# Four graph layers on one core: a tenth buffer for the token tile, the value bias moved into a shared buffer, and a new order of the same instructions

## The chip, the cores and the metric

The kernel runs on one core of one Trainium2 chip. The metric is the device time of one launch in microseconds (us). The core has a matrix engine (TensorE, PE in the profile), three engines for elementwise work (VectorE or DVE, ScalarE or ACT, GpSimd or POOL) and a queue (SyncE, SP) from which all transfers between memory and the core are issued. Each engine runs its own instructions in the order in which the program lists them, and waits where an operand isn't ready yet.

## The reference, cut to what matters

128 graphs of 64 nodes with 512 numbers per node pass through four layers. Each layer normalizes its input, applies ReLU, mixes the nodes of a graph with a 64 x 64 matrix made from `adj`, multiplies by weights, and adds the result to the input.

```python
# layer 0
h = jnp.maximum(_layernorm(x), 0.0)
x = x + _L0_gnn_ref(h, adj, ...)      # two hypergraph convolutions, 512 -> 1024 -> 512
# layer 1
h = jnp.maximum(_layernorm(x), 0.0)
x = x + _L1_gnn_ref(h, adj, ...)      # A @ h @ w, A from tanh, exp and row sums
# layer 2
h = jnp.maximum(_layernorm(x), 0.0)
x = x + _L2_gnn_ref(h, adj, ...)      # weight = adj * exp(query keyt); weight @ value
#    value = h @ Wv_w.T + Wv_b        <- the bias "bv" of this text
# layer 3
h = jnp.maximum(_layernorm(x), 0.0)
x = x + _L3_gnn_ref(h, adj, ...)      # H = sum over k of (transition^k h) @ Wk[k] + bk[k]; relu
```

## The kernel before

The 8192 nodes are cut into 16 groups of four tiles of 128 nodes. The first half of the program takes every group through layers 0 and 1 and stores the four x tiles to memory (`xm`); the second half loads them again and takes every group through layers 2 and 3. The weights of the second half are loaded over those of the first when these are no longer needed.

The program isn't written in the order in which it runs. Each operation is put into a graph with an engine, a rough cost and a priority. A list scheduler then walks the graph with its own rough clock, gives every buffer a place out of a fixed number when its first operation starts, and lists each engine's instructions in the order that this walk found. Transfers wait for a place to come free.

```python
SLOTS = {
    "x": ([P, D], 9), "adj": ([P, 2, T, C], 3), "h": ([P, D], 5), "o": ([P, D], 2),
    ...
}
TWO = [                                   # the same memory, first half / second half
    ([("tmp", [P, D], 4), ("mB", [P, T, C + 1], 1)], [("s3", [P, 3, 6, P], 1)]),
    ...
    ([("y", [P, D], 2)], [("qT", [P, 2, 2 * P], 2)]),
    ...
]
```

A place on the right side of `TWO` can be given out only when all uses of the left side are over. Where the scheduler's clock shows a gap of over half a microsecond on TensorE, and a PSUM buffer is free, it puts in matmuls of ones whose result nobody reads (fills), so that the engine doesn't stand still:

```python
    gap, (since, i) = t - at["PE"], min(free["ps"], default=(t, 0))
    if o.eng == "PE" and gap > 0.5 and since <= at["PE"]:
        fills.append((o.seq, slots["ps"][i], gap))
...
def fill(ps, gap):
    for _ in range(int(gap * FILL / (0.224 if filled else 0.448))):
        nc.tensor.matmul(ps[:, :P], ones, ones, start=True, stop=True)       # L1013
    filled.append(gap)
```

An fp32 matmul of the program is two instructions in the profile. The priorities of an operation are a running count (`G.prio`), which grows by a period per group and by stretches within a layer, plus an offset per part of a layer (`AT`):

```python
STRETCH, PERIOD1, PERIOD2 = (2.11, 6.43, 4.5, 0.21), 79.8, 140.53
AT = {"x0": -1458.56, "apart": 58.27, "w1": -1207.06, ...}
def part(name):
    G.shift = AT[name]
```

Products of a weight with a pair of tiles are done in seven block products in place of eight (Strassen-Winograd): `strassen` makes sums of tile blocks on VectorE and then multiplies.

```python
def comb(d, kd, x_, kx, y_, ky, op):                                     # L599
    dve(c_v(kc * P), lambda: nc.vector.tensor_tensor(d(), x_(), y_(), op), [*kx, *ky], kd)
...
            nc.tensor.matmul(p.t[:, :n], lhsT()[:, c, :], rhs(c), ...)   # L607 (layer 2: L845)
...
comb(s1, ...); comb(s2, ...); comb(a[1, 0], ...); comb(s4, ...)
seven({1: prod(a11), 2: prod(a12), 3: prod(s4), 4: prod(a22), 5: prod(s1), 6: prod(s2), 7: prod(a21)}, U, n, emit)
```

The seven products run in the order 1, 6, 7, 2, 5, 4, 3. Four quarters of the result come out after the 2, the 5, the 4 and the 3. Some lines that the profile names (cut; line numbers are those of the kernel before):

```python
dma(256, lambda: nc.sync.dma_start(xx.t, at), key, [xx])                 # L344 x of a tile
pe(..., q_ @ k_, ...)                                                    # L467 Wq times Wk, set-up
nc.vector.bn_stats(st.t[:, i, :], src(i))                                # L516 mean, variance
nc.scalar.activation(h.t, xx.t, AF.Relu, bias=nm.t, scale=rs.t)          # L537 h of a tile
nc.tensor.matmul(quad(p)[:, c, :], h.t[...], rhs(), ...)                 # L546, copied by L548
nc.scalar.copy(planes, src)                                              # L555 before a DMA transpose
nc.sync.dma_start_transpose(back, planes)                                # L556, copied by L557
nc.tensor.matmul(pmv()[:, t, :], HT.t[:, t, :], mB.t[:, t, :], ...)      # L705 layer 0's node matrix
nc.tensor.matmul(pf.t, M.t[:, t, :], y.t, ...)                           # L758 end of layer 0, reads y
nc.vector.tensor_mul(PT.t[s, :, s], z.t[s], by_node(rn, s))              # L787 layer 1's node matrix
nc.tensor.matmul(quad(pl)[s, ...], hT.t[...], q()[...])                  # L878 logits of layer 2
nc.tensor.matmul(p.t, PT.t[:, t, :], v_.t[:, t % 2, c0:c1])              # L911 layer 2's output
nc.vector.transpose(tt.t[...], tr.t[...])                                # L948 layer 3's node matrix
nc.tensor.matmul(p2.t[...], tr.t[:, t, :], tt.t[:, t, 0, :])             # L957 its square
nc.tensor.matmul(quad(pqs[k][i])[:, c, :], hh[k].t[half, ...], tt...)    # L973
nc.vector.scalar_tensor_tensor(xx.t[:, cols], U.t[:, iv], 0.0, xx.t[:, cols], ...)  # L992 end of layer 3
dma(256, lambda: nc.sync.dma_start(out[r:r + P, :], xx.t), ...)          # L995
```

The bias of v has a buffer of its own, loaded once. It is used in layer 2 alone:

```python
bv_b = const.tile([P, D], F32, name="bv_b")
dma(256, lambda: nc.sync.dma_start(bv_b, bv.partition_broadcast(P)), [], ["bv_b"])    # L1055
```

Of the kernel before, what the change touches and what calls it, by code (L numbers as in the profile page):

```python
# [8 lines left out]
F32 = mybir.dt.float32  # L9
# [5 lines left out]
P = 128  # L15
C = 64
D = 512
DH = 1024
T = 4
# [148 lines left out]
def tile_adj_preln_d4(  # L168
# [6 lines left out]
    nc = tc.nc  # L175
# [3 lines left out]
    const = ctx.enter_context(tc.tile_pool(name="const", bufs=1))  # L179
# [3 lines left out]


    SLOTS = {
        "x": ([P, D], 9), "adj": ([P, 2, T, C], 3), "h": ([P, D], 5), "o": ([P, D], 2),
        "u5": ([P, 3, D], 2), "u2": ([P, 3, D // 2], 1),
        "bd": ([P, T, P], 4), "rw": ([P, C, T], 1), "ee": ([P, T, C], 2),
        "st": ([P, 2, 6], 6), "mv": ([P, 2], 10), "ve": ([P, 1], 10), "rs": ([P, 1], 10), "nm": ([P, 1], 10),
# [5 lines left out]
        ([("z", [P, DH], 2)], [("hT", [P, KD, T * P], 1)]),  # L195
        ([("rT", [P, KH, P], 3)], [("vu", [P, 2, D + 1], 2), ("tt", [P, T, 2, C], 2)]),
        ([("s2", [P, 3, 4, P], 1), ("s1", [P, 3, 2, P], 2)], [("a3", [P, 3 * KD, P], 2)]),
        ([("y", [P, D], 2)], [("qT", [P, 2, 2 * P], 2)]),
        ([("mT", [P, KD, P], 3)], [("a3", [P, 3 * KD, P], 1)]),
        ([("row", [P, D], 4)], [("sh", [P, 4, 2, 2 * P], 1)]),  # L200
        ([("wa", [P, D], 1)], [("q", [P, D], 1)]),
# [5 lines left out]
    def size(shape):  # L207
        n = 1
        for d in shape[1:]:
            n *= d  # L210
        return n

    for two in TWO:
        both = work.tile([P, max(sum(size(shape) * n for _, shape, n in tags) for tags in two)], F32,
                         name="_".join(tag for tags in two for tag, _, _ in tags))
        for tags in two:
            at = 0
            for tag, shape, n in tags:
                for i in range(n):
                    v = both[:, at:at + size(shape)]  # L220
                    at += size(shape)
                    if len(shape) == 3:
                        v = v.rearrange("p (a b) -> p a b", a=shape[1])
                    elif len(shape) == 4:
                        v = v.rearrange("p (a b c) -> p a b c", a=shape[1], b=shape[2])
# [30 lines left out]
    def c_v(n, from_psum=False):  # L256
        return n / 960 + 0.155 + 0.05 * from_psum
# [4 lines left out]
    def dve(cost, fn, r, w):  # L262
        return G.op("DVE", cost, fn, r, w)
# [4 lines left out]
    def pool(cost, fn, r, w):  # L268
        return G.op("POOL", cost, fn, r, w)

    def dma(kb, fn, r, w, issue=0.34):
        return G.op("SP", max(kb / 380.0, issue), fn, r, w)

    def quad(b):
# [2 lines left out]
    FILL = 0.75  # L277


    STRETCH, PERIOD1, PERIOD2 = (2.11, 6.43, 4.5, 0.21), 79.8, 140.53  # L280
    AT = {
        "x0": -1458.56, "apart": 58.27, "w1": -1207.06, "b1": -1268.61, "w2": 312.2, "w": -214.25, "c1": 103.95,
        "l0": -1592.46, "c2": -560.69, "l1": 125.29, "c": 849.04, "g0": -1279.86, "g1": -1456.39, "g2": -589.08,
        "g3": -1259.16, "g": -1258.76, "bq": 321.93, "l3": 56.2, "wg": 1603.23, "w3": 387.13, "beg0": -72.8,
        "beg1": 73.58, "end00": 0.51, "end01": 19.09, "end11": -75.14, "new2": 31.64, "new3": 4.77, "end2": -39.58,
        "end3": -21.31, "load1": -108.19, "load2": 27.97, "m": 12.29, "h0": 9.53, "p0": 10.98, "z0": -29.14,
        "q0": 15.48, "y0": -518.61, "h1": -26.33, "p1": -22.59, "z1": -30.25, "q1": 4.48, "y1": -2.94, "s": -20.64,
        "t0": -25.67, "e0": -522.9, "t1": -42.32, "e1": -53.88, "hT": 8.77, "sh": 220.05, "lq": 8.14, "pt": -124.53,
        "v": 35.92, "pv": -915.5, "s3": 19.84, "tt": -865.12, "a0": 46.62, "b0": -371.48, "a1": 104.26, "b1_": 198.72,
    }  # L290

    def part(name):
        G.shift = AT[name]
# [31 lines left out]
    def load_tmp(tag, n, shape_of, src):  # L325
        b = Buf(tag)
        dma(n * P * 4 / 1024, lambda: nc.sync.dma_start(shape_of(b.t), src), [], [b])
        return b
# [74 lines left out]
    def combine_hT(name, w_, x_, left):  # L403

        blk = lambda i, j: w_[:, 2 * i:2 * i + 2, j * D // 2:(j + 1) * D // 2]
        low, high = [(name, 0)], [(name, 1)]
        V = name + "V"
        add, sub = nc.vector.tensor_add, nc.vector.tensor_sub  # L410
        f = lambda i: (lambda c, o=slice(0, D // 2): x_[:, i, c, o])
        b = lambda i, j: (lambda c, o=slice(0, D // 2): blk(i, j)[:, c, o])
        v = lambda fn, r, w: dve(c_v(D), fn, r, w)
        if left:
            v(lambda: add(x_[:, 0], blk(0, 1), blk(1, 1)), [*low, *high], [(name, "x0")])
            v(lambda: sub(x_[:, 1], x_[:, 0], blk(0, 0)), [*low, (name, "x0")], [(name, "x1")])
            v(lambda: sub(x_[:, 2], blk(1, 0), x_[:, 1]), [*high, (name, "x1")], [(name, "x2")])
            v(lambda: sub(blk(0, 1), blk(0, 0), blk(0, 1)), [*low, (name, "x0")], [V])
        else:
            v(lambda: add(x_[:, 1], blk(1, 1), blk(0, 1)), [*low, *high], [(name, "x1")])  # L420
            v(lambda: sub(blk(0, 1), blk(0, 0), blk(0, 1)), [*low, (name, "x1")], [V])
            v(lambda: sub(x_[:, 0], blk(1, 1), blk(0, 1)), [*high, V], [(name, "x0")])
            v(lambda: sub(x_[:, 2], blk(1, 0), x_[:, 0]), [*high, (name, "x0")], [(name, "x2")])
        N = name + "N"
        v(lambda: nc.vector.tensor_scalar(blk(1, 1), blk(1, 1), -1.0, None, op0=ALU.mult), [*high, (name, "x0"), (name, "x1")], [N])
        x = lambda i: (f(i), [(name, f"x{i}")])
        if left:
            return {1: (b(0, 0), low), 2: (b(1, 0), high), 3: x(2), 4: (b(1, 1), [N, *high]), 5: x(0), 6: x(1), 7: (b(0, 1), [V])}
        return {1: (b(0, 0), low), 2: (b(1, 0), high), 3: (b(1, 1), [N, *high]), 4: x(2), 5: (b(0, 1), [V]), 6: x(0), 7: x(1)}
# [103 lines left out]
    def pre_ln(g, t, stats=None):  # L533

        xx, h = xt[g, t], Buf("h")
        nm, rs = stats or pre_stats(g, t)
        act(0.82, lambda: nc.scalar.activation(h.t, xx.t, AF.Relu, bias=nm.t, scale=rs.t), [xx, nm, rs], [h])  # L537
        return h
# [271 lines left out]
    def layer2(g):  # L810
        ad = adjs[g]
        part("hT")
        hT = Buf("hT")
        hk = [(hT, t) for t in range(T)]
        for t in range(T):
            h = pre_ln(g, t)
# [16 lines left out]
        pair = lambda f: f.rearrange("p (a n) -> p a n", a=2)  # L833
# [58 lines left out]

        def emit_v(i, j, p, u, v):
            cols, at = slice(j * D // 2, (j + 1) * D // 2), slice(j * (D // 2 + 1), j * (D // 2 + 1) + D // 2)
            bias = bv_b[:, None, cols].to_broadcast([P, 2, D // 2])
            add, ka = (lambda: bias), "bv_b"
            if u is not None:
                (U, iu), iv = u, v[1]
                pool(1.3, lambda: nc.gpsimd.tensor_add(pair(U.t[:, iv]), pair(U.t[:, iu]), bias), [u, "bv_b"], [v])
                add, ka = (lambda: pair(U.t[:, iv])), v  # L900
            dve(c_v(D), lambda: nc.vector.tensor_add(vb[i].t[:, :, at], pair(p.t), add()), [p, ka], [(vb[i], j)])


        hv = {**hs, 3: hs[4], 4: hs[3], 5: hs[7], 7: hs[5]}
        seven({n: prod(WV[n], hv[n], False) for n in range(1, 8)}, Buf("u5"), D, emit_v)
        PTk = [(PT, 0), (PT, C)]
        part("pv")
        for t in range(T):
# [6 lines left out]
            for j in range(2):  # L915
                cols = slice(j * D // 2, (j + 1) * D // 2)
# [134 lines left out]
    load_w("wg", wg_sb, wg_d, olds("w1", KD), ["wg_d"])  # L1051
    load_w("wv", wv_sb, WvT, olds("w1", KD))
    WG, WV = combine_hT("wg", wg_sb, wg_x, True), combine_hT("wv", wv_sb, wv_x, False)
    bv_b = const.tile([P, D], F32, name="bv_b")
    dma(256, lambda: nc.sync.dma_start(bv_b, bv.partition_broadcast(P)), [], ["bv_b"])  # L1055
    part("w3")
    for k in range(3):
        src = Wk3[k].rearrange("(c p) o -> p c o", p=P)
# [49 lines left out]
def _program(arrays, n_tokens):  # L1108
    import concourse.bacc as bacc

    nc = bacc.Bacc("TRN2", target_bir_lowering=False, num_devices=1)
    args = [nc.dram_tensor(f"in_{k}_dram", arrays[f"in_{k}_dram"].shape, F32, kind="ExternalInput").ap()
            for k in _NAMES]
    args.append(nc.dram_tensor("out_0_dram", (n_tokens, D), F32, kind="ExternalOutput").ap())
    with tile.TileContext(nc) as tc:
        tile_adj_preln_d4(tc, *args)
    return nc
# [12 lines left out]
```

## Time and profile before

| what | before |
|---|---|
| median of 3 runs | 2374.7 us (2371.99 to 2375.38) |
| span of the profiled execution | 2373.3 us |
| instructions | 33860 |
| DVE, ACT, POOL busy | 73%, 53%, 40% |
| bytes moved | 171.02 MB, mean 72 GB/s |
| granted TensorE clock, mean | 0.997 |

The page gives each engine's busy time and its share of the span. A table by stretches of time gives the same numbers for any part of the span, also for the instructions of one source line alone. The list of waits says which engine stood still until which instruction of another engine was done, in total, how often, and the longest. A timeline lists instructions of one engine in order of time, neighbours of the same kind merged: start, duration, engine, line, operation, output and inputs, count, and in brackets the idle time ahead of it and what ended it. "Idle" on TensorE and the fills together are the time in which the engine does nothing for the result.

### The profile page before, as it was taken

To read this page: it belongs to the slowest core of one execution; us is meant where nothing else is said; L and a number is where in the kernel's file an instruction comes from. 1 tells how busy PE (TensorE), PEld (TensorE's weight loads), DVE (VectorE), ACT (ScalarE), POOL (GpSimd) and SP (SyncE) were. 2 spreads that over 40 slices of the span, in tenths; PEclk is the share of its full clock that TensorE was granted. 3 is DMA by queue.
4 is the path that set the end of the run, shared out by engine and by line. 5 is a ranking of instruction groups with operands and counts; after the bars stand their busy time and mean duration, and the time that the engine had idled before them with its cause. 6 is when DMAs were issued, how large, how long until landed. Compare 5 with 4: busy or idle time off the path is not lost.

```text
span 2373.3 us, 33860 instructions
## 1 busy us (share of the span) xinstructions
PE 2349.7 (99%) x12008; PEld 1867.5 (79%) x12008; DVE 1742.1 (73%) x3798; ACT 1268.7 (53%) x1746; POOL 958.7 (40%) x1514
## 2 busy tenths in 40 slices
PE   9999999999999999999999999999999999999999
PEld 4677677777677776677788888888888888888887
DVE  7888778788778788777868566666666766667764
ACT  4566656567565576565745445444445444454422
POOL 6244455544455444555443323333323333323330
PEclk9999999999999999999999999999999999999999
DMA  7333222333223333232532322213322223322211
GB/s 258 80 80 65 54 68 64 71 80 63 50 68 69 72 80 54 55 73 71 133 106 59 76 69 61 69 45 69 76 64 65 64 52 73 71 63 65 48 36 40
DMA packets 336922, 171.02 MB, mean 72 GB/s; under 512 B 284656, under 2 KB 290672, under 8 KB 336752
## 3 DMA queue, kind: packets, MB, share of 16 engines
q1 hardware_dynamic: 336752, 168.86, 29.5%
q8 instruction: 94, 1.54, 0.3%
q14 instruction: 76, 0.62, 0.1%
HBM read 66.99 MB, written 34.70 MB: 43 GB/s over the span
## 4 chain that ended last, share of the span: by engine, by line
PE 89%; DVE 5%; DMA 3%; ACT 1%; issue 1%; POOL 1%; SPq 1%; DVEq 0%; ACTq 0%
PE ps L607 61%; PE ps L845 14%; PE ps L546 4%; PE ps L911 2%; PE ps L758 2%; PE ps L973 2%; PE ps L878 1%; DMA x<-xm 1%; DVE st L516 1%; PE ps L957 0%; DMA rw<-row 0%; PE ps L705 0%; DVE tmp_mB_s L599 0%; DVE o L381 0%; PE ps L467 0%
## 5 line engine op out<-in xcount | busy, mean ns | idle before, releaser
L537 ACT ACTIVATE h<-x,nm,rs 128x512 f32<-128x512 f32 x384 | 300.2, 810 | 399.6 <-POOL nm L524 366.8
L607 PE MATMUL ps<-wb_mem,s_s_a 128*128 128x256 f32 x2184 | 512.0, 380 | 0.3
L607 PEld LDWEIGHTS ps<-wb_mem,s_s_a 128*128 128x128 f32 x2184 | 409.5, 190 | 74.0 <-issue 19.8
L518 POOL TENSOR_SCALAR rs<-mv 128x1 f32<-128x1 f32 x320 | 99.2, 310 | 493.0 <-DVE mv L517 477.5
L607 PE MATMUL ps<-wb_mem,tmp_mB_s 128*128 128x256 f32 x1152 | 262.4, 380 | 3.2 <-DVE tmp_mB_s L599 3.1
L607 PEld LDWEIGHTS ps<-wb_mem,tmp_mB_s 128*128 128x128 f32 x1152 | 218.1, 190 | 35.3 <-DVE tmp_mB_s L599 5.4
L607 PE MATMUL ps<-wb_mem,mT_a 128*128 128x256 f32 x1016 | 242.0, 380 | 0.0
L607 PE MATMUL ps<-wa_mem,mT_a 128*128 128x512 f32 x512 | 237.3, 595 | 3.9 <-ACT mT_a L548 3.9
L607 PE MATMUL ps<-wb_mem,rT_vu_tt 128*128 128x256 f32 x1024 | 238.2, 380 | 0.6 <-ACT rT_vu_tt L557 0.6
L607 PEld LDWEIGHTS ps<-wb_mem,rT_vu_tt 128*128 128x128 f32 x1024 | 192.8, 191 | 41.3 <-issue 12.5
L607 PEld LDWEIGHTS ps<-wb_mem,mT_a 128*128 128x128 f32 x1016 | 192.2, 190 | 31.8 <-issue 5.7
L516 DVE BATCH_NORM_STATS2 st<-x 128x6 f32<-128x512 f32 x256 | 173.6, 678 | 45.8 <-DMA x<-xm 40.6
L519 POOL TENSOR_TENSOR rs<-rs,mhalf 128x1 f32<-128x1 f32 x320 | 193.3, 604 | 26.4
L607 PEld LDWEIGHTS ps<-wa_mem,mT_a 128*128 128x128 f32 x512 | 97.1, 190 | 112.7 <-issue 102.4
L607 PE MATMUL ps<-wa_mem,s_s_a 128*128 128x512 f32 x384 | 180.7, 593 | 0.3 <-DVE z_hT L627 0.3
L987 POOL TENSOR_TENSOR u<-u,bk_b 128x256 f32<-128x256 f32 x96 | 76.4, 796 | 238.9 <-DVE u L579 170.2
L575 ACT COPY u<-ps 128x256 f32<-128x256 f32 (+1 forms) x160 | 72.7, 454 | 177.8 <-PE ps L845 105.1
L635 POOL TENSOR_TENSOR u<-u,row_sh 128x256 f32<-128x256 f32 x96 | 74.9, 789 | 228.1 <-DVE u L577 211.6
L733 ACT ACTIVATE z_hT<-z_hT 128x512 f32<-128x512 f32 x128 | 79.6, 627 | 157.8 <-DVE z_hT L627 157.8
L557 ACT COPY rT_vu_tt<-z_hT 128x1024 uint16<-128x1024 uint16 x128 | 147.1, 1159 | 13.7 <-DMA z_hT<-tmp_mB_s 13.3
L546 PEld LDWEIGHTS ps<-bd,h 128*128 128x128 f32 x1024 | 131.1, 192 | 26.6 <-issue 22.2
L524 POOL TENSOR_SCALAR nm<-mv,rs 128x1 f32<-128x1 f32 x320 | 138.5, 433 | 31.1
(174 smaller groups left out, 4336.0 us busy)
## 6 DMA issues: line engine op xcount, KB each, us to landing
x<-in_x_dram SPq DMA_DIRECT2D x64, 256.0 KB, 2.7
xm<-x SPq DMA_DIRECT2D x64, 256.0 KB, 2.1
x<-xm SPq DMA_DIRECT2D x64, 256.0 KB, 2.8
out_dram<-x SPq DMA_DIRECT2D x64, 256.0 KB, 2.0
adj<-in_adj_dram SPq DMA_DIRECT2D x32, 256.0 KB, 4.0
rw<-row SPq DMA_DIRECT2D x94, 64.0 KB, 2.8
wb_mem<-in_Wk_dram SPq DMA_DIRECT2D x6, 512.0 KB, 5.3
tmp_mB_s<-in_Wk_dram SPq DMA_DIRECT2D x8, 256.0 KB, 3.1
```

Source lines behind the costliest of these rows:

```text
L516: dve(0.69, lambda i=i: nc.vector.bn_stats(st.t[:, i, :], src(i)), [r[i]], [(st, i)])
L518: pool(0.32, lambda: nc.gpsimd.tensor_scalar_add(rs.t, mv.t[:, 1:2], EPS), [mv], [rs])
L519: pool(0.65, lambda: nc.gpsimd.tensor_tensor(rs.t, rs.t, mhalf, ALU.pow), [rs], [rs])
L524: pool(0.47, lambda: nc.gpsimd.tensor_scalar(nm.t, mv.t[:, 0:1], rs.t, -1.0, op0=ALU.mult, op1=ALU.mult), [mv, rs], [nm])
L537: act(0.82, lambda: nc.scalar.activation(h.t, xx.t, AF.Relu, bias=nm.t, scale=rs.t), [xx, nm, rs], [h])
L546: nc.tensor.matmul(quad(p)[:, c, :], h.t[:, c * P:(c + 1) * P], rhs(), start=True, stop=True)
L557: act(1.16, lambda: nc.scalar.copy(u16(dst()).rearrange("p c (k q) -> p c k q", q=2), u16(back()).rearrange("p (q c r) -> p c r q", q=2, c ...
L607: nc.tensor.matmul(p.t[:, :n], lhs()[:, c, :], rhs(c), start=first and c == 0, stop=c == kc - 1, skip_group_check=True)
L635: pool(0.75, lambda: nc.gpsimd.tensor_add(U.t[:, iv], U.t[:, iu], row()[:, cols]), [u, krow], [v])
L733: act(0.63, lambda: nc.scalar.activation(z.t[:, cols], z.t[:, cols], AF.Relu), [(z, j)], [(z, j)])
L845: nc.tensor.matmul(pair(p.t)[:, o, :], a, b, start=first and o == 0 and c == 0, stop=c == 1, skip_group_check=True)
L987: pool(0.88, lambda: nc.gpsimd.tensor_add(U.t[:, iv], U.t[:, u[1]], add()), [u, ka], [v])
```

## The change

Three things are changed. The x tiles of 128 nodes get ten places instead of nine. The bias of v no longer has memory of its own for the whole program: it is loaded into memory that holds `y` in the first half, where `qT` gives up one of its two places. The 2 KB per partition that come free are those that the tenth x place takes. And the constants that set the priorities are all new, so the same operations are listed in another order on every engine and in the transfer queue.

```diff
-        "x": ([P, D], 9), "adj": ([P, 2, T, C], 3), "h": ([P, D], 5), "o": ([P, D], 2),
+        "x": ([P, D], 10), "adj": ([P, 2, T, C], 3), "h": ([P, D], 5), "o": ([P, D], 2),
...
-        ([("y", [P, D], 2)], [("qT", [P, 2, 2 * P], 2)]),
+        ([("y", [P, D], 2)], [("qT", [P, 2, 2 * P], 1), ("bv", [P, D], 1)]),
...
-    STRETCH, PERIOD1, PERIOD2 = (2.11, 6.43, 4.5, 0.21), 79.8, 140.53
+    STRETCH, PERIOD1, PERIOD2 = (2.17, 8.2, 5.0, 0.93), 74.41, 150.73
     AT = {
-        "x0": -1458.56, "apart": 58.27, "w1": -1207.06, "b1": -1268.61, "w2": 312.2, "w": -214.25, "c1": 103.95,
...
+        "x0": -1535.64, "apart": 75.57, "w1": -1233.0, "b1": -1087.63, "w2": 841.47, "w": -80.41, "c1": 385.12,
...          (all 59 offsets have new values)
-            bias = bv_b[:, None, cols].to_broadcast([P, 2, D // 2])
-            add, ka = (lambda: bias), "bv_b"
+            bias = lambda: bv_b.t[:, None, cols].to_broadcast([P, 2, D // 2])
+            add, ka = bias, bv_b
...
-    bv_b = const.tile([P, D], F32, name="bv_b")
-    dma(256, lambda: nc.sync.dma_start(bv_b, bv.partition_broadcast(P)), [], ["bv_b"])
+    bv_b = load_tmp("bv", D, lambda t: t, bv.partition_broadcast(P))
```

## The prediction

> **What bounds the kernel now.** I read the page first, for the engine that is full.
>
> ```profile
> PE 2349.7 (99%) x12008; PEld 1867.5 (79%) x12008; DVE 1742.1 (73%) x3798; ACT 1268.7 (53%) x1746; POOL 958.7 (40%) x1514
> ```
>
> TensorE is busy for 99% of the span, and no other engine for more than 73%. The change adds and removes no useful instruction on it, so all that it can win is time in which TensorE stands still or does fills. I therefore cut the span into stages and asked for each engine's busy time in them, and then for the fills alone (line 1013).
>
> ```profile
> 0.00:100.00 100.00, 91.89 (x309) 51.67 (x310) 80.53 (x159) 46.25 (x68) 47.74 (x70) 0.97 0.63 194
> 100.00:1100.00 1000.00, 999.01 (x4238) 726.03 (x4237) 801.61 (x1773) 631.34 (x874) 487.89 (x775) 1.00 0.29 67
> 1100.00:1300.00 200.00, 195.38 (x1064) 159.46 (x1063) 154.98 (x328) 109.27 (x147) 85.16 (x134) 0.99 0.36 91
> 1300.00:2300.00 1000.00, 995.56 (x6030) 870.66 (x6029) 668.35 (x1457) 461.77 (x629) 326.06 (x515) 1.00 0.27 64
> 2300.00:2373.30 73.30, 67.84 (x374) 59.65 (x373) 36.61 (x85) 20.08 (x29) 11.87 (x21) 0.97 0.13 37
> ```
>
> The first number after the stretch is its length, the next TensorE's busy time. The same table for the fills alone:
>
> ```profile
> 0.00:100.00 100.00, 6.62 (x34) 6.19 (x34) 0.97 0.63 194
> 100.00:1100.00 1000.00, 0.83 (x6) 0.83 (x6) 1.00 0.29 67
> 1100.00:1300.00 200.00, 10.24 (x86) 10.23 (x86) 0.99 0.36 91
> 2300.00:2373.30 73.30, 4.62 (x38) 4.48 (x38) 0.97 0.13 37
> ```
>
> Idle plus fills by stage: start 8.11 + 6.62 = 14.7 us; first half 0.99 + 0.83 = 1.8; change of halves 4.62 + 10.24 = 14.9; second half 4.44; end 5.46 + 4.62 = 10.1. The sum, 45.9 us, is all there is to win, 1.9% of the time. Some of it can't be won: the first data have to come (TensorE's first useful matmul starts at 8.8 us), and after the last matmul (2369.3) lie the last sums and the store, 4.0 us. The first half runs as dense as it can: its groups follow each other every 71.77 us (starts of line 705 in the timeline). In the second half the period is 71.27 us where nothing is late (starts of line 878), and 7 of 12 periods are longer, by 4.7 us in all.
>
> The lists of waits, asked by stage, say what ended the stalls:
>
> ```profile
> PE ps L607 <- ACT mT_a L548: 3.9, 1, 3.9
> PE ps L607 <- DVE tmp_mB_s L599: 3.1, 4, 1.1
> DVE st L516 <- DMA x<-xm: 40.6, 16, 4.3
> ```
>
> The first is in the start, the other two in the second half. VectorE waits 16 times for an x tile that is loaded only when a place is free, and as it works in order, the block sums behind that wait (L599) come late to TensorE. At the end:
>
> ```profile
> 2317.18 0.65 PE L667 MATMUL ps<-ee,ones 64*64 64x256 f32 x4
> 2317.76 2.86 PE L607 MATMUL ps<-wb_mem,tmp_mB_s 128*128 128x256 f32 x12
> 2320.45 3.96 PE L1013 MATMUL ps<-ones 128*128 128x128 f32 x34
> 2325.85 1.10 PE L957 MATMUL ps<-rT_vu_tt,bd 128*128 128x64 f32 x8 [1.44 <-DVE rT_vu_tt L948]
> 2327.42 5.41 PE L973 MATMUL ps<-rT_vu_tt,h 64*128 64x128 f32 x64
> ```
>
> The last group's chain from L667 to L957 takes 8.7 us on VectorE, with one product (2.6 us) to cover it. The 64 matmuls of L973 then take 5.41 us; the same 64 took 3.84 in the middle of the second half.
>
> [...]
>
> **The change part by part.** *Bias of v.* The early load falls away, one of 256 KB comes at the change of halves. In the new transfer order it stands behind the last reads of `y`, as its place demands; the transfers behind it are late weights and that same group's next steps, which need those reads too. It is first needed about 30 products later. Cost 0. *One qT place.* A group writes one qT and the logits read it; the next group writes its own a period later. Cost 0.
>
> *Order, end.* In the new list the fills there are 3 matmuls instead of 19, and four products (4 x 2.6 = 10.4 us) instead of one lie between L667 and L957. That covers 8.7 us. Removed: fills 4.6 - 0.7 (6 halves of about 0.12) = 3.9, idle 1.4, slow L973 5.41 - 3.84 = 1.6, together 6.9. I keep 0.9 for a new short wait: -6.
>
> *Order, change of halves.* Fills are 27 matmuls instead of 43. Most (24) stand in one place: ahead of the first L546 of the last group's layer 1. From the last L758 (ends 1184.2) to the second L787 (ends 1207.4) that chain took 23.2 us. The old list covers it with layer 2 products; L546 starts at 1208.1 without waiting. The new list has four L546 (3.5) and fourteen short L607 (14 x 0.86 = 12.1) there: 15.6 us covered, 7.6 not. In return the two layer 2 blocks that stood apart by fills of 3.51 and 4.63 us are joined. Estimate after: 7.6 + 0.5 (other fills) + 2.5 (waits like those before, which were 4.6) = 10.6, against 14.9; a percent of slow clock in 200 us, 2 us before, shrinks by about one. -5.
>
> *Order, start.* Fills 19 against 17 (and 3 more soon after 100 us). Wq and Wk go first, but layer 0's first matmuls come behind the set-up product instead of ahead of it, and the fourth x tile, which their operands now wait for on VectorE, is the tenth transfer. I count one product less done by about 62 us: +1. On the other side the three L548 copies, which stood behind an L555 that waited for a `tmp` place until 68.8 us, are now listed ahead of every L555: of the 3.9 us, -3. Net -2.
>
> *Tenth x place, second half.* Adding up VectorE's mean durations between the last L992 on an x place and the L516 on its next tile gives 4.0, 5.9, 1.6, 1.6 us for a group's four tiles before and 4.3, 7.2, 1.4, 3.0 after. Store (2.0) and load (2.8, both from the page) have to fit there, with VectorE's own idle time. So some waits stay. But only one tile's L516 instead of two now stands right ahead of block sums, and it follows the last-but-one product. TensorE then has about 13.6 us of other work (2.6 for the last product, 0.9 for L957, 2.1 for L878, 2.0 for half of L973, two L845 of 1.73, 2.6 for the next first product) against 10.7 before, for a chain of about 11.4 (two sums and their update 1.7 + 1.5, store, load and issue 5.5, statistics and two block sums 2.7). -3 of 4.7.
>
> Sum: -6 - 5 - 2 - 3 = -16. The order was made with rough costs, and a list that is new everywhere can have a late operand that I don't see. I give back 2: 2374.7 - 14 = 2361.
>
> **The rivals.** *A new wait per group.* First-half groups have nothing to lose now; if each of 14 lost 1 us to a copy or sum that comes late, the gain would be gone: 2375. For it: all offsets are new, VectorE is 80% busy there. Against it: the new list puts no fill anywhere in the first half after the start. *The x place does nothing.* The shortest distance is 1.4 us, less than 1.6. Then 2364. *All inner gaps close.* Take 45.9 us, leave 8.8 at the start and 4.0 at the end: 2374.7 - 33.1 = 2342. Against it are the 27 fills at the change of halves and the uncovered 7.6 us. *The start gets worse*, by the first chain's lateness and no gain on L548: +3 instead of -2, 2366.
>
> **Range and chances.** The two sure parts (end, fewer fills at the change of halves) give 2364 alone; the rivals spread from 2342 to 2375 with most weight on small misses either way: 2353 to 2369. Faster by 2% would need 2327, below what is left when every gap closes: 0.5%. Slower by 2% needs 48 us of new stalls: 1%.
>
> **What would show it.** Fills 98 halves instead of 164, of which 6 at the end; L973 of the last group in about 4 us; one stretch of fills of about 5.4 us at the change of halves, ended by L787; periods of 71.77 and 71.27 again, with the second half's excess below 2 us; no long wait on L548 in the start. I am wrong if a period of either half grows, if the wait for `x<-xm` reaches TensorE as often as before, or if the start loses more than 17 us.

## The result and the profile after

The changed kernel takes 2386.6 us (median of 5 runs, 2385.5 to 2393.1), the kernel before 2374.7: a ratio of 1.0059, 95% interval 1.0040 to 1.0077. It is slower by about 12 us; 14 us less had been forecast. The profiled execution of after is the longest of the five (span 2391.3 us), so its losses below are some 6 us larger than those of the median run.

First the page's line of engines, after (before stands in the prediction):

```profile
PE 2348.4 (98%) x11942; PEld 1859.5 (78%) x11942; DVE 1795.3 (75%) x3798; ACT 1266.2 (53%) x1746; POOL 979.6 (41%) x1514
```

VectorE executes 3798 instructions in both kernels, the same ones in another order, and needs 1795.3 us for them instead of 1742.1. That is the line to stop at: the forecast had taken their durations to be the same in any order. Now the table by stages, after; the columns are the stretch, its length, then busy time and instructions of PE, PEld, DVE, ACT and POOL, granted clock, DMA share and GB/s:

```profile
0.00:100.00 100.00, 85.19 (x266) 43.43 (x267) 79.32 (x147) 40.08 (x60) 48.85 (x66) 0.93 0.59 190
100.00:1100.00 1000.00, 986.82 (x4133) 707.18 (x4132) 821.76 (x1735) 618.03 (x856) 483.81 (x759) 1.00 0.29 64
1100.00:1300.00 200.00, 193.71 (x1005) 156.91 (x1004) 152.21 (x319) 114.14 (x153) 86.45 (x140) 0.99 0.40 101
1300.00:2300.00 1000.00, 995.36 (x6044) 875.76 (x6043) 696.07 (x1503) 466.95 (x640) 347.20 (x528) 1.00 0.27 63
2300.00:2391.30 91.30, 87.34 (x503) 76.21 (x501) 45.95 (x98) 26.99 (x40) 13.30 (x22) 0.99 0.15 44
```

The fills alone (line 1014 now; from line 200 on, after's lines are one higher than before's):

```profile
0.00:100.00 100.00, 7.48 (x38) 6.92 (x38) 0.93 0.59 190
1100.00:1300.00 200.00, 5.91 (x50) 5.90 (x50) 0.99 0.40 101
1300.00:2300.00 1000.00, 0.66 (x4) 0.53 (x4) 1.00 0.27 63
2300.00:2391.30 91.30, 0.94 (x6) 0.74 (x6) 0.99 0.15 44
```

| idle + fills of TensorE, us | before | forecast | after |
|---|---|---|---|
| start, 0 to 100 | 14.7 | 12.7 | 14.8 + 7.5 = 22.3 |
| first half, 100 to 1100 | 1.8 | 1.8 | 13.2 + 0 = 13.2 |
| change of halves, 1100 to 1300 | 14.9 | 10 | 6.3 + 5.9 = 12.2 |
| second half, 1300 to 2300 | 4.4 | 1.4 | 4.6 + 0.7 = 5.3 |
| end | 10.1 | 4 | 4.0 + 0.9 = 4.9 |
| sum | 45.9 | 30 | 57.9 |

The forecast column counts about 1 us of slow clock at the change of halves and 1.6 us at the end as if they were idle time. The gain of the end arrives, that of the change of halves in part; the first half and the start lose far more. (The sum grows by 12.0 us, the two profiled spans differ by 18.0. The other 6 are TensorE's busy time without fills, 2327.4 before and 2333.4 after, for the same matmuls. In the start the granted clock is 0.93 instead of 0.97, which makes about 4 us of 100; the rest isn't accounted for.)

What ended TensorE's waits in the first half, after (engine, line, releaser: us in total, times, longest):

```profile
PE ps L608 <- DVE s_s_a L600: 10.0, 18, 2.5
PE ps L759 <- DVE y_qT_bv L638: 2.8, 6, 0.8
```

So the products wait mostly for VectorE's block sums. The prediction had named a longer period of either half as a sign that it was wrong, and it came: two groups of the first half took 143.5 us before (2 x 71.77) and take 145.6 to 149.0 now (starts of L706 from 274 us on). One of these waits as the timelines of VectorE, GpSimd and TensorE show it, after (start, duration, instruction):

```profile
394.69 0.69 DVE L600 TENSOR_TENSOR s_s_a<-s_s_a,rT_vu_tt 128x512 f32<-128x512 f32 x1
395.30 1.76 DVE L600 TENSOR_TENSOR rT_vu_tt<-rT_vu_tt 128x512 f32<-128x512 f32 x1
396.98 1.75 DVE L600 TENSOR_TENSOR s_s_a<-rT_vu_tt,s_s_a 128x512 f32<-128x512 f32 x1
398.65 1.48 DVE L600 TENSOR_TENSOR s_s_a<-mT_a 128x256 f32<-128x256 f32 x1
400.17 0.43 DVE L600 TENSOR_TENSOR s_s_a<-s_s_a,mT_a 128x256 f32<-128x256 f32 x1
```

```profile
395.21 1.30 POOL L723 TENSOR_TENSOR x<-x,h 128x512 f32<-128x512 f32 x1 [0.43 <-ACT h L538]
396.58 1.60 POOL L724 TENSOR_TENSOR x<-x,row_sh 128x512 f32<-128x512 f32 x1
398.14 1.71 POOL L723 TENSOR_TENSOR x<-x,h 128x512 f32<-128x512 f32 x1
```

```profile
400.65 1.98 PE L608 MATMUL ps<-wa_mem,s_s_a 128*128 128x512 f32 x4 [2.14 <-DVE s_s_a L600]
```

The sum at 394.69 takes 0.69 us. The next three run beside three additions of GpSimd and take 1.76, 1.75 and 1.48; once GpSimd is done, the fifth takes 0.43 again. The additions are stretched too, to 1.60 and 1.71 us. TensorE pays 2.14. Sorting every L599/L600 sum of both traces by whether it overlaps a wide GpSimd addition: sums of 128x256 take 417 ns free in before and 416 in after, 943 and 938 beside one; 38 of 256 lie so before, 61 after. Of the 128 sums of 128x512, 28 do before and 46 after; free they take 682 and 677, beside one up to 1202 before and 1761 after. Standing beside an addition doesn't always lengthen a sum: of those 28 in before, one took over 800 ns; the others started ahead of the addition or in its last 0.19 us. Counting only lengthened sums, over 500 ns for 128x256 and over 800 for 128x512, there are 28 before and 75 after.

The traces show how the lengthened ones end. The sums that start at 395.30 and 396.98 each end 0.55 us after the addition that was running when they started (396.51 and 398.18), so most of a sum, 0.68 us when free, fits behind that addition. All 28 lengthened sums of before and all 75 of after are like this: each started while a wide addition ran, and ended 0.55 us after it when it is of 128x512 (31 of them in after), 0.28 us after it when it is of 128x256 (44). Why, the traces don't show. The theory to be tested: *the new order puts more block sums beside GpSimd's additions; a sum that starts during one (a collision) is done only behind it, the sums come late, and TensorE waits.* Rivals: the order itself lists an operand too late; the places or the bias cost something; GpSimd's work is too long for its new place.

### The profile page after: what moved, and what is told of

Read it like the earlier page. It is cut to its first block, busy times and chain, and to the rows that moved or that the text cites. A ratio compares the mean times of both kernels' runs of the same rounds, so it can differ in the third digit from the quotient of the medians.

```text
span 2391.3 us, 33612 instructions
## 1 busy us (share of the span) xinstructions
PE 2348.4 (98%) x11942; PEld 1859.5 (78%) x11942; DVE 1795.3 (75%) x3798; ACT 1266.2 (53%) x1746; POOL 979.6 (41%) x1514
## 4 chain that ended last, share of the span: by engine, by line
PE 75%; DVE 12%; DMA 7%; POOL 3%; issue 2%; ACT 1%; SPq 1%; DVEq 0%; ACTq 0%; POOLq 0%
PE ps L608 51%; PE ps L846 12%; PE ps L547 3%; DVE s_s_a L600 2%; PE ps L912 2%; PE ps L974 2%; PE ps L759 2%; DVE st L517 1%; DMA rw<-row 1%; DMA xm<-x 1%; DVE o L382 1%; POOL nm L525 1%; PE ps L879 1%; DMA row<-col 1%; DMA x<-xm 1%
## 5 line engine op out<-in xcount | busy, mean ns | idle before, releaser
L538 ACT ACTIVATE h<-x,nm,rs 128x512 f32<-128x512 f32 x384 | 306.1, 813 | 360.0 <-POOL nm L525 241.8
L525 POOL TENSOR_SCALAR nm<-mv,rs 128x1 f32<-128x1 f32 x320 | 143.3, 448 | 30.8
L800 POOL TENSOR_TENSOR x<-x,u 128x256 f32<-128x256 f32 x96 | 83.4, 892 | 151.9 <-DVE u L578 92.7
L578 DVE TENSOR_TENSOR u<-ps,u 128x256 f32<-128x256 f32 (+1 forms) x160 | 84.2, 526 | 77.4 <-PE ps L608 56.6
L556 ACT COPY o<-h 128x1024 uint16<-128x1024 uint16 x128 | 133.3, 1042 | 13.2 <-DMA wa_q<-o 8.2
```

The costliest lines, as they stand in the source:

```text
L525: pool(0.47, lambda: nc.gpsimd.tensor_scalar(nm.t, mv.t[:, 0:1], rs.t, -1.0, op0=ALU.mult, op1=ALU.mult), [mv, rs], [nm])
L556: act(1.05, lambda: nc.scalar.copy(u16(planes.t).rearrange("p (q c) -> p q c", q=2), u16(src()).rearrange("p (c q) -> p q c", q=2)), ksrc, ...
L578: dve(c_v(n), lambda: nc.vector.tensor_add(at(1)(), p2.t[:, :n], at(0)()), [p2, (U, 0)], [(U, 1)])
L800: pool(0.75, lambda: nc.gpsimd.tensor_add(xx.t[:, cols], xx.t[:, cols], U.t[:, iu]), [xx, u], [xx])
```

## The experiments

Ratios are to the kernel before, run beside each version on the same chip, with 95% intervals. The versions ran in four sets, in which the medians of before were 2375.9, 2372.5, 2376.4 and 2375.9 us, so across sets ratios are compared, not times. Idle times are those of one profiled execution each.

**Bias and qT place alone.** The kernel before with its own constants and nine x places:

```diff
-        ([("y", [P, D], 2)], [("qT", [P, 2, 2 * P], 2)]),
+        ([("y", [P, D], 2)], [("qT", [P, 2, 2 * P], 1), ("bv", [P, D], 1)]),
-    bv_b = const.tile([P, D], F32, name="bv_b")
+    bv_b = load_tmp("bv", D, lambda t: t, bv.partition_broadcast(P))
```

> The kernel before with its own constants, so its order unchanged, but v's bias in the place of y and one qT place; nine places for x. Both theories of the loss (order, or the collisions that the order brings) expect no change here: 2373 to 2377, ratio 0.999 to 1.001. If the bias or the lost qT place costs anything, it shows at the change of halves (idle and fills there were 14.9 us) or as a longer period of the second half (71.27 us), and the time comes near 2380.

Measured: 2374.7 us, 0.9995 (0.9986 to 1.0003); change of halves 14.5 us of idle and fills, second half 4.1. These places cost nothing that shows. The tenth x place couldn't be tried alone: with the old offsets and ten places the list comes to a point where no operation finds a free place, and with the new offsets and nine places it holds 312 fill matmuls instead of 49; neither was run.

**No reading of SBUF by GpSimd in layers 0 and 1.** After's order, instruction for instruction on the other engines; the sums of GpSimd are left out:

```diff
-nc.gpsimd.tensor_add(xx.t, xx.t, h.t)
+(nc.gpsimd.memset(xx.t, 0.0), nc.gpsimd.memset(xx.t, 0.0))     # likewise x+b2, u+bias, x+u
```

> The kernel after, same order, but the four GpSimd additions of layers 0 and 1 (x+h, x+b2, u+bias, x+u) are replaced by two memsets of the same tile each, so GpSimd is still busy for about two thirds of the time but reads nothing from SBUF; the sums are left out of the result. [...] VectorE's block sums fall back from a mean of 736 ns to at most 660, VectorE's busy time from 1795 us by at least 40, the first half's idle time (13.2 us from 100 to 1100) to 2 to 5, the start's 22.3 to about 17: 2368 to 2376. Rival, the order itself lists an operand too late on VectorE or PE: 2383 to 2388, the idle time of 100 to 1100 stays above 10. Rival, GpSimd's additions are only too long for the order: between the two, about 2378, with the waits on x from GpSimd gone and block sums as long as before.

Measured: 2362.5 us, 0.9943 (0.9931 to 0.9956); VectorE 1719 us, first half 0.3 us of idle, start 15.1. All three go the way that the theory had them, and further: the time is below its range. The granted clock from 100 to 1100 us is 1.00 with and without the additions, so the first half's gain doesn't come from a faster clock. No sum of 128x256 or 128x512 is lengthened any more.

**The same in the kernel before, as a control.**

> Control: the same four GpSimd additions replaced by two memsets each in the kernel before. [...] VectorE's busy time falls from 1742 us by 30 to 60, but the first half loses only 1.8 us there, so the time stays within 2370 to 2376. If this kernel falls by as much as the one with the order after does (over 8 us), the additions cost both orders the same and the theory doesn't explain the difference.

Measured: 2369.2 us, 0.9969 (0.9956 to 0.9981), just below the expected range; VectorE 1710 us. The old order gains 6 to 7 us, four of them in the start (14.7 to 10.9), none in the first half. The four are the wait on L548: it is gone although the order is the same, and the L555 ahead of that copy starts at 63.0 us instead of 68.8. The new order gains about 27 (1.0059 to 0.9943). So the additions cost the two orders very differently, and without them the new order is the faster one.

**Is it the additions themselves, or that the memsets are shorter?** Three memsets each instead of two:

```diff
+[nc.gpsimd.memset(xx.t, 0.0) for _ in range(3)]     # in place of each of the four additions
```

> As the run with two memsets, but three for each of the four additions of layers 0 and 1, so that GpSimd is busy for at least as long as with the additions (3 x 0.52 = 1.57 us against 1.47, 3 x 0.31 = 0.93 against 0.89), still without reading SBUF. [...] as with two memsets, 2361 to 2366. Rival, what counted there was that GpSimd's work was shorter: most of the 24 us comes back, 2378 to 2387.

Measured: 2361.8 us, 0.9957 (0.9945 to 0.9969). GpSimd is now busier than in after (1008 against 980 us), and TensorE loses only 1.1 us in the first half. The stretch from 100 to 1100 (columns as above), and the same five sums in this run, VectorE and then GpSimd:

```profile
100.00:1100.00 1000.00, 998.88 (x4227) 723.69 (x4226) 776.60 (x1769) 634.94 (x877) 516.00 (x1318) 1.00 0.29 66
```

```profile
382.34 0.69 DVE L600 TENSOR_TENSOR s_s_a<-s_s_a,rT_vu_tt 128x512 f32<-128x512 f32 x1
382.95 0.69 DVE L600 TENSOR_TENSOR rT_vu_tt<-rT_vu_tt 128x512 f32<-128x512 f32 x1
383.55 0.68 DVE L600 TENSOR_TENSOR s_s_a<-rT_vu_tt,s_s_a 128x512 f32<-128x512 f32 x1
384.16 0.42 DVE L600 TENSOR_TENSOR s_s_a<-mT_a 128x256 f32<-128x256 f32 x1
384.61 0.42 DVE L600 TENSOR_TENSOR s_s_a<-s_s_a,mT_a 128x256 f32<-128x256 f32 x1
```

```profile
382.84 1.69 POOL L723 MEMSET x<- 128x512 f32 x3 [0.40 <-ACT h L538]
384.59 1.69 POOL L724 MEMSET x<- 128x512 f32 x3
```

GpSimd is as busy beside them as before, but it reads nothing, and every sum has its free duration. So it isn't the length of GpSimd's work. What the runs show is that additions lengthen the sums and memsets of the same length don't; what it is in an addition that does it, its reads or something else, they don't show.

**Shorter pieces.** Nothing left out; the two additions of 128x512 in halves:

```diff
+[nc.gpsimd.tensor_add(xx.t[:, c:c + 256], xx.t[:, c:c + 256], h.t[:, c:c + 256]) for c in (0, 256)]
```

> The kernel after, with GpSimd's two additions of 128x512 in layer 0 (x+h, x+b2) cut into two of 128x256 each, nothing left out. If VectorE has to wait for the one running GpSimd instruction only, its waits halve there (0.73 instead of 1.27 us each) and the first half's idle time falls by some 3 to 6 us: about 2381. [...] nothing is won, and GpSimd is longer by 128 x 0.2 = 25 us: 2386 or worse.

Measured: 2386.8 us, 1.0040 (1.0027 to 1.0054); inconclusive, its interval overlaps after's. First half 10.4 us of idle instead of 13.2; but the next version, in which layers 0 and 1 are untouched, has 10.4 too, so this difference is no gain. A 128x256 sum beside an addition now takes 792 ns instead of 938 on average, at most 983 instead of 1530, but 94 of them meet one instead of 61. So the sums are lengthened by less, and more of them are: 102 instead of 75. GpSimd is busy for 1015 us instead of 980.

**The second half's additions alone.** The three of layers 2 and 3 (biases of q, v, k) become two memsets each, their sums are left out; layers 0 and 1 as in after.

> The kernel after; only the three GpSimd additions of layers 2 and 3 (bias of q, bias of v, bias of k) are replaced by two memsets of the same tile each, the sums are left out; layers 0 and 1 are untouched. [...] the loss sits in the start and the first half, so here VectorE's busy time falls by 20 to 40 us, the second half's 5.3 us of idle and fills by at most 2, and the time stays at 2384 to 2387. If the collisions of the second half reach TensorE too, and not the late x tile or ScalarE's copies, its idle falls below 2 us: about 2381.

Measured: 2378.8 us, 1.0028 (1.0019 to 1.0038), so about 7 us less than after. My expectation was wrong, the rival in it right: the second half's idle falls from 4.6 us to 0.4, the change of halves from 12.2 to 9.4. The first half, which isn't touched, shows 10.4 instead of 13.2 with the same 75 lengthened sums: so much do stages of single executions differ. The lists of waits had misled me. After's second half showed waits on ScalarE's copies, not on sums:

```profile
PE ps L608 <- ACT mT_a L979: 2.0, 2, 1.4
PE ps L608 <- ACT s_s_a L979: 1.8, 2, 1.5
DVE st L517 <- DMA x<-xm: 53.5, 17, 5.0
```

and without the collisions:

```profile
PE ps L608 <- ACT mT_a L979: 0.4, 1, 0.4
DVE st L517 <- DMA x<-xm: 41.1, 16, 5.3
```

The last updates of x (L993, L992 in before), from which an x place comes free, also read two tiles, and their mean duration goes the same way. In before, in after and here (the mean in ns is the second number after the bar):

```profile
L992 DVE SCALAR_TENSOR_TENSOR x<-u,x 128x256 f32<-128x256 f32 x128 | 55.9, 437 | 4.4
L993 DVE SCALAR_TENSOR_TENSOR x<-u,x 128x256 f32<-128x256 f32 x128 | 75.1, 587 | 4.4
L993 DVE SCALAR_TENSOR_TENSOR x<-u,x 128x256 f32<-128x256 f32 x128 | 54.4, 425 | 4.4
```

VectorE's wait for x tiles is back at 41.1 us from 53.5, near the 40.6 of before.

**The additions on VectorE.** Nothing left out; VectorE does x+h, or x+h and x+b2, at the place in the list where GpSimd had them:

```diff
-nc.gpsimd.tensor_add(xx.t, xx.t, h.t)
+nc.vector.tensor_add(xx.t, xx.t, h.t)         # second run: x+b2 too
```

> The kernel after, nothing left out; x+h of layer 0 is given to VectorE, at the place in the common list where GpSimd had it, so no other order changes. It takes half of the long GpSimd additions of layer 0 away, for 64 x 0.68 = 44 us more of VectorE[...]. [...] the first half's idle falls from 13.2 to about 6 and the start by some 3: 2374 to 2380. Rival, VectorE is too full (85% of the first half) and waits in its order for ScalarE's h: 2386 or more.

> The same with x+h and x+b2 both given to VectorE: no 128x512 addition of GpSimd is left in the first half. [...] first half's idle 1 to 4, start 16 to 19, 2364 to 2372, faster than both kernels. Rival, VectorE is too full: 88 us more work in the first half, it becomes the late one, 2380 or more.

Measured: 2384.5 us, 1.0045 (1.0033 to 1.0057), and 2381.7, 1.0034 (1.0021 to 1.0047). First half 9.3 and 7.4 us of idle, start 21.5 and 19.1. The direction fits the theory, but the size is a third of what was expected, both intervals overlap that of after, and the second time lies in the range of the rival, a VectorE that is too full. The two can't be told apart here. VectorE is busy for 1801 and 1809 us, 6 and 14 more than in after for some 44 and 88 us of added work, so most of the stretching is gone; but that work now stands in VectorE's own list, and the 128x256 additions are still on GpSimd.

**No wide GpSimd addition at all, new order and old.** The replacements of the three-memset run and of the second-half run together.

> The kernel after with all seven kinds of wide GpSimd additions (four in layers 0 and 1, three in layers 2 and 3) replaced by memsets of the same tiles, sums left out: the new order without any wide GpSimd instruction that reads SBUF. If the gains of the runs on each half add up (0.9957 and 1.0028 against 1.0059 of the kernel after): 1.0059 - 0.0102 - 0.0031 = 0.9926, 2355 to 2359 us; the first half's idle below 1.5, the second half's below 1, VectorE's busy time near 1675. If both runs took away the same loss, it stays at 2361 to 2364.

> The same replacement in the kernel before: the old order without such instructions. If its second half's 4.4 us of idle come from the x tiles that are late, as the prediction had it, nothing more is won than in the control for layers 0 and 1 (0.9969): 2366 to 2370. If collisions cause them, as in the kernel after, they go too: 2362 to 2365. The difference to the same run of the new order is what the order is worth without collisions; the prediction had put it at 14 us, the runs on the first half alone gave 6.7.

Measured: new order 2358.3 us, 0.9930 (0.9918 to 0.9943); old order 2365.6, 0.9963 (0.9950 to 0.9977). The new order's time is as expected: the gains add up. Its idle times are not: 3.8 us in the first half and 1.1 in the second, against 1.5 and 1 at most. The old order's time lies between its two ranges. Idle and fills by stage: new 14.9, 3.8, 11.0, 2.0, 4.3; old 12.0, 2.0, 13.2, 3.5, 10.1. The old order's second half keeps most of its loss (waits on L599 2.9 us, five times, and VectorE waiting for x 17 times), so there the late x tile seems to be a cause of its own. Without collisions the new order is worth 7.3 us.

**Orders with fewer collisions.** Only the constants are changed, nothing is left out: the new order with ten places, the old one with nine and the bias in the place of y.

```diff
-"h0": 12.42, ... "z0": -87.88, ... "z1": 104.16, ... "load2": 398.21      # after
+"h0": 28.98, ... "z0": -6.49, ... "z1": 76.8, ... "load2": 137.49         # most others by less
```

> The kernel after, nothing left out, same places; its constants moved so that fewer of VectorE's sums with two SBUF inputs come to stand beside a wide GpSimd addition (h0 from 12 to 29, z0 from -88 to -6, and small moves of most others; fills 51 matmuls instead of 49). [...] the order can be mended by order alone; the first half's idle falls from 13.2 to about 6, the end and the second half stay as they are: 2368 to 2376, near the kernel before or a little faster. If the collisions only move elsewhere: 2382 or more.

> The run with the bias in the place of y and nine x places, nothing left out, with the old constants moved in the same way. Its first half loses only 1.8 us to begin with, the collisions cost it about 9 us in all by the runs without them (2374.7 against 2365.6): 2369 to 2373 if a third to a half of that can be had by order alone, 2375 if not.

Measured: new order 2381.8 us, 1.0026 (1.0015 to 1.0036); old order 2372.1, 0.9984 (0.9976 to 0.9992). In the new one the first half's 13.2 us become 2.2 of idle and 1.9 of fills, a little better than the 6 expected, by order alone and with every addition in its place. Lengthened sums fall from 75 to 38 there, and in the old order from 28 to 16. The time of the new one misses the expected 2376 at most and lies next to the rival's 2382, although the collisions have not just moved; the start has stayed at 22.5 us. It is faster than after all the same: the two intervals don't overlap. The old order's first half goes from 1.8 to 0.2 us. It has the lowest ratio of the versions that leave nothing out, 3.8 us below the kernel before; its interval overlaps that of the bias and qT places alone.

## Why the prediction was wrong

**First half, forecast 0, measured +11.4: the step that failed.** "First-half groups have nothing to lose now", and "the new list puts no fill anywhere in the first half". A fill shows where the list's own costs leave a gap. Those costs know nothing of sums that get longer beside an addition, so the absence of fills says nothing of this loss. The working took durations from rows of the kernel before as if they belonged to an instruction; they belonged to its neighbours too. The row means of before held the hint: 128x256 sums of the same kind in four groups with means of 583, 511, 450 and 438 ns. The rival "a new wait per group" had the right place and nearly the size (1 us for each of 14 groups, with 2375 as the result), and I dismissed it on the fills.

**Start, forecast -2, measured +7.6.** The L548 wait is gone, as said, but its place in the list was not all that had caused it: in the old order it goes too when GpSimd's additions go (the control above). New losses come instead; the start loses 22.3 us with all additions and 14.9 without any. The two longest waits there, after:

```profile
PE ps L468 <- DMA tmp_mB_s<-in_Wk_dram: 4.3, 2, 3.5
PE ps L451 <- DVE tmp_mB_s L449: 3.4, 1, 3.4
```

The second falls to 0.5 us without the additions of layers 0 and 1. Even without any wide addition the new start is 2.9 us worse than the old one (14.9 against 12.0). The lateness was put at +1; the wait for loads of Wk stands in all runs of the new order, with 4.1 to 4.9 us, against 0.2 in before. The start lost more than 17 us, the other sign of being wrong.

**Tenth x place, forecast -3 of 4.7, measured +0.9.** The estimate of TensorE's cover set a chain of free durations against it. With collisions L993 got longer, and VectorE waited 17 times for 53.5 us in this stretch instead of 16 times for 40.6; that the first led to the second is likely, not shown. Without any collision the second half loses 2.0 us in the new order and 3.5 in the old. The sign was right there, the size half. What the place does apart from the order stays open, as the two couldn't be separated.

**Change of halves, forecast -5, measured -2.7.** The fills are as said: one stretch of 5.52 us, ended by L788. The waits were put at 2.5 us and measured 6.3; without collisions they are 4.4, the sum 11.0 against the 10.6 of idle and fills in the forecast. The granted clock of the stretch is 0.99 in both. The mechanism was right, the new waits in it were mis-sized.

**End, forecast -6, measured -5.2 of idle and fills, and 1.6 less for L974.** The parts came as forecast: 6 fill halves, no wait ahead of L958, and the last group's 64 matmuls of L974 in 3.84 us instead of 5.41. The granted clock is 1.00 while L974 runs. In before it was 0.50 from 2327.4 to 2330.7 and 1.00 in the 3.4 us ahead of that; L973's pairs follow every 0.21 us until 2330.8 and every 0.11 after it. What lowered it isn't shown. Fills run until 2324.4, eight matmuls of L957 follow from 2325.85, four more fill halves from 2326.8, and L973 starts at 2327.4; the longest standstill is 1.44 us. That the new order is what kept the clock up isn't shown either: with the old order and the bias in the place of `y`, the end has the same 38 fill halves and 10.0 us of idle and fills, and its granted clock is 1.00 instead of 0.97.

```profile
2338.28 1.00 PE L958 MATMUL ps<-rT_vu_tt,bd 128*128 128x64 f32 x8
2347.04 3.84 PE L974 MATMUL ps<-rT_vu_tt,h 64*128 64x128 f32 x64
```

**Bias and qT, forecast 0, measured 0.9995.** Right.

Taken together: the order's worth without collisions is 7.3 us, half of the 14 forecast. The collisions cost the old order about 9 us and the new one about 28 (2374.7 and 2386.6 against their runs without wide additions; 9 and 31 by the ratios). The difference of the two, 19 less 7.3, is the 12 us of the result; this is the same subtraction in another order, not a further proof. Between the two profiled executions of the new order, idle and fills account for 22.0 us; another 13.6 are busy time of the same matmuls (2333.4 and 2319.8 without fills), while the mean granted clock is 0.996 with the additions and 0.999 without, which is some 7 us of it. So what VectorE delivers late shows only in part as idle time of TensorE.

## What to carry to other kernels

When an order is changed, compare the mean duration of each kind of instruction before and after, not only the waits: the same count with a longer busy time (here 1742.1 to 1795.3 us on VectorE, 958.7 to 979.6 on GpSimd) was the sign of the collisions, and a list made from fixed costs can't see them. A replacement that keeps an engine busy but takes away what it reads (a memset in place of an addition) helped here to tell additions that lengthen the sums beside them from too much work. A gain read from a list is only as good as the durations under it; ask of each dense engine what runs beside it in the new order.

## What was not expected of the hardware

A VectorE sum of two SBUF tiles of 128x256 took 416 ns alone and, on average, 938 beside GpSimd's additions; one of 128x512 took 677 alone and up to 1761. GpSimd's addition of 128x512 was stretched as well, from 1.30 to 1.71 us in the example shown. Memsets of GpSimd lengthened no sum of layers 0 and 1 (with three memsets, 457 ns at most for 128x256 and 705 for 128x512). In the second half TensorE waited for ScalarE's copies by the list of waits, and its idle time fell from 4.6 us to 0.4 when the additions there were gone: here the list named the last link, not the cause.
